# Memsets between indirect gathers: one of 512 elements behind every fourth gather instead of one of 128 behind each

## The chip, the core and the metric

The kernel runs on one core of a Trainium2 chip. The metric is the device time of one execution in microseconds (us). Lower is better. One execution was also recorded by the hardware profiler; the views below come from it. Engines are named as the profile names them: PE is TensorE, PEld its weight loads, DVE is VectorE, ACT is ScalarE, POOL is GpSimd, SP is SyncE, which here issues most of the plain transfers.

## The reference

A graph network of two attention layers with a layer norm ahead and a residual around it, on 6250 nodes of 256 features. There are 200000 edges, sorted by destination, with 32 features each. All data is float32. Cut to what matters:

```python
def _gat(x, src, dst, ea, Wg, a_s, a_d, Wge, a_e, b, n, h, f):
    hx = (x @ Wg).reshape(n, h, f)
    he = (ea @ Wge).reshape(-1, h, f)
    al = leaky_relu(einsum(hx, a_s)[src] + einsum(hx, a_d)[dst] + einsum(he, a_e), 0.2)
    m = segment_max(al, dst, num_segments=n)
    al = exp(al - m[dst])
    al = al / segment_sum(al, dst, num_segments=n)[dst]
    out = segment_sum(hx[src] * al[:, :, None], dst, num_segments=n)
    return out.reshape(n, h * f) + b

def _forward(x, edge_index, edge_attr, ...):
    src, dst = edge_index
    orig = x
    te = relu(edge_attr @ We0 + be0) * exp(x @ Wo0 + bo0)[src][:, None]
    s2, d2, ea2 = _add_self_loops(src, dst, te, n)
    x = relu(_gat(x, s2, d2, ea2, Wg0, ..., n, HEADS, PH) + x)      # 4 heads of 64
    te = relu(edge_attr @ We1 + be1) * exp(x @ Wo1 + bo1)[src][:, None]
    s2, d2, ea2 = _add_self_loops(src, dst, te, n)
    x = _gat(x, s2, d2, ea2, Wg1, ..., n, 1, D) + x                 # 1 head of 256
    return x + orig

h = maximum(_layernorm(x, axis=-1), 0.0)
x = x + _forward(h, edge_index, edge_attr_32, ...)
```

What the change touches is `hx[src]`: for each edge, the row of its source node is fetched from memory.

## The kernel before

The prologue normalises the nodes and writes a table `T` with one row per node: the node's 256 transformed features and a few numbers that the logits need (266 values in all in layer 0). While it does so, 24 gathers of the plain `x` rows (L243) fill the buffer `G0` for the first step; no memset follows these.

The 200000 edges are cut into 1563 chunks of 128, one edge per partition. A step has C = 24 chunks; a layer has 66 steps, of which the last two have 14 and 13 chunks. All edges of a step are sorted by destination, so its sums belong to at most 128 destination rows. The loop in `edges` goes over the steps of both layers. Its iteration k emits, in this order: the loads of the destination rows of step k+2 (`nodes`, L989), the load of the local row numbers `lb` of step k+2, now and then a load of further edge indices, the gathers of step k+1 (`gather`, L916), the logits and maxima of step k, the parts of step k+1 that depend on the edge features (`rphase1`, `rphase2`; L1014, L1019, L1028), the load of the edge features `ea` of step k+2, the scaling of the gathered rows by their weights (L1223), the sums (L1234), the one-hot matrices of the next step (L1058), the finish of step k-1 (`finish`, with the stores of rows to `T` or to the output in `rows3`), the eviction of the sums from PSUM (L1239), and the carry to the next step (L1245).

**The gathers.** `gather` issues one indirect transfer per chunk on Pool. Each fetches 128 rows of `T` into one slot of `G`, the last chunk's first, then chunks 0, 1, 2 and so on. `G` has three buffers that steps take in turn, so the first gather of a batch waits until the sums of an earlier step have read the buffer. Every gather also waits for the one that used its semaphore eight gathers before. Behind each gather, except in step 0, Pool writes zeros to a tile `gap` of 128 elements per partition (L932). Nothing reads `gap`.

**The sums.** For each chunk, a matmul of the one-hot matrix `S` (edges by destination rows) with the scaled rows `G` adds to one PSUM tile `u`: 24 in a step, 48 records in the profile. ScalarE then copies `u` to `U` (L1239). A step's end is told below by this copy.

**The destination rows.** `nodes` reads a row number into a register of SP and loads the 128 destination rows of a step from `T`, and in layer 0 those of `x` too, into the tile `tw` (522 elements per partition, five buffers). The row is loaded two steps ahead, and read last in the finish of its step, one iteration behind it. SP issues its transfers in the program's order. What stands behind `nodes` in SP's queue is `lb`, the index loads, the flags `fl`, the edge features `ea` and the row stores.

At the end of a layer, the last steps are emitted by `begin`, `tight` and `last` in an order of their own; in layer 1's first step, several batches of gathers follow each other without a pause.

Of the kernel before, what the change touches and what calls it, by code (L numbers as in the profile page):

```python
# [22 lines left out]
F32 = mybir.dt.float32  # L23
# [8 lines left out]
P = 128  # L32
# [3 lines left out]
D = 256  # L36
# [42 lines left out]
class Kernel:  # L79
# [317 lines left out]
    def fixed_rows(self):  # L397
        nc, cp = self.nc, self.cp
        self.crow = cp.tile([1, D + self.L[0].H], F32, name="crow")
        self.cl = [cp.tile([36, P + 1], F32, name=f"cl{i}") for i in range(2)]  # L400
        for t in self.cl:
            nc.gpsimd.memset(t, -BIG)

        self.cnt = cp.tile([P, self.NS, 2], F32, name="cnt")
        self.mt = cp.tile([P, 4 * C + 4], F32, name="mt")
        self.gap = cp.tile([P, 128], F32, name="gap")
        self.fb = [cp.tile([P, 37 * C], F32, name=f"fb{i}") for i in range(2)]
        for t in [self.mt] + self.fb:
            nc.gpsimd.memset(t, 0.0)


        self.aq = [cp.tile([P, 4, 32], BF, name=f"aq{i}") for i in range(2)]
        for t in self.aq:
            nc.gpsimd.memset(t, 0.0)
        self.trow1 = []
        L1 = self.L[1]
        for i in range(2):
            self.trow1.append(cp.tile([P, 2 * L1.TW], F32, name=f"t1row{i}"))
            nc.gpsimd.memset(self.trow1[i][:, L1.TW + D:], 0.0)
# [498 lines left out]
    def gather(self, st, c0=0, idx=None):  # L918
        nc, L = self.nc, st["L"]
        st["G"] = G = self.G0 if st["k"] == 0 else self.gp[st["k"] % 3].tile([P, C, 270], F32, name="G")  # L920
        n = self.N
        if idx is None:
            idx = self.src[:, st["o"]:st["o"] + st["C"]]
        else:
            n += P
        last = st["C"] - 1
        for c in (range(c0, last + 1) if c0 else (last, *range(last))):
            nc.gpsimd.indirect_dma_start(  # L928
                out=G[:, c, 0:L.TW], out_offset=None, in_=self.rows[L.l][0:n * (1 + L.l), :],
                in_offset=bass.IndirectOffsetOnAxis(ap=idx[:, c:c + 1], axis=0))  # L930
            if st["k"]:
                nc.gpsimd.memset(self.gap, 0.0)  # L932

    def pair(self, k):
# [54 lines left out]
    def nodes(self, st):  # L989
        nc, L, s = self.nc, st["L"], st["s"]  # L990
        r = self.row(0, s)
        tw = self.np_.tile([P, self.L[0].TW + D], F32, name="tw", bufs=5)
        st["tw"], st["xw"] = tw[:, :L.TW], tw[:, L.TW:L.TW + D]
        w = L.TW + L.l * D
        nc.sync.dma_start(tw[:, :w], self.T[L.l][ds(r, P), 0:w])
        if L.l == 0:
            nc.sync.dma_start(st["xw"], self.a["x"][ds(r, P), :])
# [402 lines left out]
    def general_layer(self, L, wp, pp):  # L1400
# [94 lines left out]
        with tc.For_i(0, full, P) as i:  # L1495
            nodes(i)
        if full < N:
            nodes(N - P)
# [98 lines left out]
```

## Time and profile before

| | |
|---|---|
| median of 3 runs | 4717.75 us (4715.25 to 4721.8) |
| the profiled execution | 4718.23 us |
| span of the recorded instructions in it | 4716.0 us |
| mean granted clock of TensorE | 0.732 |
| busy: POOL | 3701.8 us, 78% of the span |
| busy: PE / PEld | 3214.2 us, 68% / 1915.8 us, 41% |
| busy: DVE | 2878.5 us, 61% |
| busy: ACT | 574.2 us, 12% |
| gathers of L928 | 3102, 0.959 us each on Pool |
| memsets of L932 | 3102, 0.221 us each on Pool |
| one step, eviction to eviction | 34.6 us in layer 0, 34.4 us in layer 1 |

Some 2.2 us of the profiled execution lie outside its span. A row of the timeline is: start in us from the span's start, duration in us, engine, line, operation, the tile written and the tiles read, the shapes, the number of instructions in a row, and in brackets how long the engine had stood before it and what ended that. "issue" means that nothing in the profile was being waited for; "remote" means that the releaser was not among the recorded instructions. A row of the page's groups is: line, engine, operation, tiles, shapes, count, then total busy time in us and mean ns of one, then the engine's total idle time just before these and what ended most of it.

### The profile page before, as it was taken

What the parts mean: (1) busy time and instruction counts of PE and PEld (TensorE: products, weight loads), DVE (VectorE), ACT (ScalarE), POOL (GpSimd) and SP (SyncE); (2) the same over time, 40 slices, a digit from 0 to 9 for tenths busy, and PEclk for the clock granted to TensorE, in tenths of its full rate; (3) what the DMA queues carried; (4) which work ended last, traced back from release to release, by engine and by line L of the source; (5) the groups of instructions that cost most, each with busy time, mean ns of one, the idle gap of its engine ahead of it and who ended that gap; (6) DMA issues with size and microseconds to landing.
All of it is one profiled execution on the core that took longest, in us unless ns stands there. A gap on an engine that the chain in (4) does not pass through costs nothing.

```text
span 4716.0 us, 38255 instructions
## 1 busy us (share of the span) xinstructions
PE 3214.2 (68%) x10176; PEld 1915.8 (41%) x10176; DVE 2878.5 (61%) x6552; ACT 574.2 (12%) x1282; POOL 3701.8 (78%) x6350
## 2 busy tenths in 40 slices
PE   7777767777677776777655666666666666656666
PEld 6444444444444443444422333434333343433334
DVE  7566767667676676766743555546455555645555
ACT  5111111111111111111100001000000100000010
POOL 5688888888888888888648888888888888888884
PEclk9677777767777777777866677777767776777778
DMA  6344444444444444444323444444444444444442
GB/s 216 111 129 126 136 122 129 134 122 135 127 134 127 124 136 123 132 131 124 107 84 104 128 118 126 125 112 127 120 127 118 126 126 111 127 118 128 118 124 63
DMA packets 236364, 584.09 MB, mean 124 GB/s; under 512 B 63097, under 2 KB 91007, under 8 KB 236073
## 3 DMA queue, kind: packets, MB, share of 16 engines
q0 software_dynamic: 150144, 422.75, 33.8%
q1 hardware_dynamic: 85579, 158.16, 10.1%
q8 instruction: 82, 1.34, 0.1%
q14 instruction: 143, 1.17, 0.1%
q10 hardware_dynamic: 416, 0.67, 0.1%
HBM read 547.11 MB, written 34.33 MB: 123 GB/s over the span
## 4 chain that ended last, share of the span: by engine, by line
DVE 40%; another core or an unknown queue 33%; PE 16%; issue 6%; ACT 4%; POOL 0%; DMA 0%; SPq 0%; DVEq 0%; ACTq 0%; POOLq 0%
DVE G L1223 16%; DVE S L1058 8%; PE y L1014 8%; PE fin L1245 3%; DVE rt L1101 2%; ACT R L1019 1%; ACT U L1239 1%; DVE ade L1104 1%; PE fin L1329 1%; PE u L1234 1%; PE lf L1138 1%; PE zad L1028 1%; DVE mt L1172 1%; DVE m L1175 1%
## 5 line engine op out<-in xcount | busy, mean ns | idle before, releaser
L928 POOL DMA_INDIRECT G<-T,src x3102 | 2974.0, 959 | 938.3 <-issue 498.2
L1234 PE MATMUL u<-G,S 128*128 128x270 f32 (+1 forms) x6252 | 1469.7, 393 | 110.3 <-issue 58.0
L1234 PEld LDWEIGHTS u<-G,S 128*128 128x128 f32 x6252 | 1186.9, 192 | 394.5 <-issue 87.1
L1245 PE MATMUL fin<-U,lsel 128*1 128x270 f32 (+1 forms) x260 | 132.8, 613 | 1143.3 <-ACT U L1239 1136.6
L1223 DVE TENSOR_TENSOR G<-G,kps 128x6144 f32<-128x6144 f32 (+2 forms) x140 | 853.3, 6100 | 0.0
L1014 PE MATMUL y<-ea,webd 64*128 64x384 f32 (+1 forms) x1056 | 754.6, 866 | 89.2 <-issue 65.5
L932 POOL MEMSET gap<- 128x128 f32 x3102 | 684.6, 221 | 4.3 <-remote 1.3
L1148 DVE TENSOR_TENSOR_SCAN cl<-fl,cl,lf 4x129 f32<-4x129 f32 (+1 forms) x130 | 61.2, 471 | 1016.6 <-PE zad L1073 994.3
L1245 PEld LDWEIGHTS fin<-U,lsel 128*1 128x1 f32 x260 | 11.1, 81 | 1202.6 <-ACT U L1239 1201.5
L1028 PE MATMUL zad<-R,wea 128*64 128x384 f32 (+1 forms) x1056 | 474.0, 816 | 0.3 <-DVE aq L1080 0.3
L1014 PEld LDWEIGHTS y<-ea,webd 64*128 64x128 f32 x1056 | 303.3, 317 | 360.3 <-issue 330.0
L1058 DVE TENSOR_TENSOR S<-kps,loc 128x3072 f32<-128x3072 f32 x132 | 436.2, 3305 | 0.0
L1019 ACT ACTIVATE R<-y,webd 128x768 f32<-128x768 f32 x260 | 232.9, 896 | 794.6 <-PE y L1014 348.3
L1028 PEld LDWEIGHTS zad<-R,wea 128*64 128x64 f32 x1056 | 160.4, 207 | 314.9 <-issue 248.5
L1239 ACT ACTIVATE U<-u 128x270 f32<-128x270 f32 (+1 forms) x132 | 51.8, 393 | 1627.1 <-remote 1585.4
L1101 DVE STREAM_TRANSPOSE rt<-zad 128x768 f32<-128x768 f32 (+1 forms) x130 | 125.0, 961 | 27.8 <-remote 15.7
L424 PE MATMUL fin<-wg,h1T 128*128 128x260 f32 x264 | 135.7, 669 | 3.2 <-ACT h1T L1331 3.2
L1043 DVE TENSOR_TENSOR lb<-lb,kps 128x1536 bf16<-128x1536 bf16 (+1 forms) x68 | 113.0, 1662 | 0.0
L424 PE MATMUL ps<-wg,hT 128*128 128x266 f32 x292 | 89.8, 435 | 25.4 <-ACT hT L311 13.9
L424 PEld LDWEIGHTS fin<-wg,h1T 128*128 128x128 f32 x264 | 76.0, 317 | 53.7 <-issue 36.3
L1272 ACT ACTIVATE mw<-mw,mg 128x2 f32<-128x2 f32 x66 | 19.7, 298 | 557.3 <-DVE mw L1264 249.1
L1138 PE MATMUL lf<-ident,fb 128*36 128x128 f32 (+1 forms) x132 | 54.9, 416 | 42.8 <-DVE al L1119 28.2
(193 smaller groups left out, 2269.0 us busy)
## 6 DMA issues: line engine op xcount, KB each, us to landing
G<-T,src POOLq DMA_INDIRECT x3102
ea<-in_ea_dram SPq DMA_DIRECT2D x64, 768.0 KB
lb<-locrow SPq DMA_DIRECT2D x64, 384.0 KB
T<-t1row SPq DMA_DIRECT2D x66, 260.0 KB
tw<-T SPq DMA_DIRECT2D x66, 258.0 KB
tw<-T SPq DMA_DIRECT2D x66, 134.0 KB
tw<-in_x_dram SPq DMA_DIRECT2D x66, 128.0 KB
out_dram<-fb SPq DMA_DIRECT2D x64, 128.0 KB
```

Of the source, the lines that this page charges most:

```text
L424: self.nc.tensor.matmul(ps[:, :L.MW], hT[:, k, :], self.wg[L.l][:, k, :], start=(k == 0), stop=(k == 1))
L928: nc.gpsimd.indirect_dma_start(out=G[:, c, 0:L.TW], out_offset=None, in_=self.rows[L.l][0:n * (1 + L.l), :], in_offset=bass.IndirectOffset ...
L932: nc.gpsimd.memset(self.gap, 0.0)
L1014: nc.tensor.matmul(y[:, o], self.webd[l][r, :], ea[r, w], start=True, stop=True)
L1019: nc.scalar.activation(R[:, i, :32 * c].rearrange("p (b n) -> p b n", b=2), y.rearrange("p (b n) -> p b n", b=2)[:, :, :16 * c], AF.Relu, ...
L1028: nc.tensor.matmul(st["zad"][i * PH:(i + 1) * PH, o], self.wea[l][0], R[:, i, w], start=True, stop=False)
L1043: V.tensor_tensor(lb[:, :, :n], lb[:, :, :n], self.k_part.unsqueeze(2).to_broadcast([P, i, n]), op=OP.is_equal)
L1058: nc.vector.tensor_tensor(st["S"][:, c0:c1, :], self.k_iota.unsqueeze(1).to_broadcast(w), self.loc[:, o + c0:o + c1].unsqueeze(2).to_broad ...
L1101: V.transpose(rv[:, :32 * c].rearrange("p (b n) -> p b n", b=2), z.rearrange("p (b n) -> p b n", b=2)[:, :, :16 * c])
L1223: nc.vector.tensor_tensor(v, v, pw[:, c0:c1, :].unsqueeze(3) .to_broadcast([P, c1 - c0, H, L.F]), op=OP.mult)
L1234: nc.tensor.matmul(st["u"][:, :L.W], S[:, i, :], G[:, i, 0:L.W], start=(j == 0), stop=(j == c - 1))
L1245: nc.tensor.matmul(pr[0:1, :L.W], self.lsel[:, s:s + 1], U[:, :L.W], start=True, stop=True)
```

## The change

The memset behind a gather is emitted only where the chunk's number leaves 3 when divided by 4, and `gap` has 512 elements per partition instead of 128. In a full batch, whose gathers go in the order 23, 0, 1, ..., 22, the memsets stand behind the gathers of chunks 23, 3, 7, 11, 15 and 19. The tile `tw` has four buffers instead of five.

```diff
-        self.gap = cp.tile([P, 128], F32, name="gap")
+        self.gap = cp.tile([P, 512], F32, name="gap")
...
             nc.gpsimd.indirect_dma_start(
                 out=G[:, c, 0:L.TW], out_offset=None, in_=self.rows[L.l][0:n * (1 + L.l), :],
                 in_offset=bass.IndirectOffsetOnAxis(ap=idx[:, c:c + 1], axis=0))
-            if st["k"]:
+            if st["k"] and c % 4 == 3:
                 nc.gpsimd.memset(self.gap, 0.0)
...
-        tw = self.np_.tile([P, self.L[0].TW + D], F32, name="tw", bufs=5)
+        tw = self.np_.tile([P, self.L[0].TW + D], F32, name="tw", bufs=4)
```

## Prediction

> **What bounds the kernel now.** I read the page first: sections 1 and 5 for Pool.
>
> ```profile
> span 4716.0 us, 38255 instructions
> ...
> PE 3214.2 (68%) x10176; PEld 1915.8 (41%) x10176; DVE 2878.5 (61%) x6552; ACT 574.2 (12%) x1282; POOL 3701.8 (78%) x6350
> ...
> L928 POOL DMA_INDIRECT G<-T,src x3102 | 2974.0, 959 | 938.3 <-issue 498.2
> L932 POOL MEMSET gap<- 128x128 f32 x3102 | 684.6, 221 | 4.3 <-remote 1.3
> ...
> L1148 DVE TENSOR_TENSOR_SCAN cl<-fl,cl,lf 4x129 f32<-4x129 f32 (+1 forms) x130 | 61.2, 471 | 1016.6 <-PE zad L1073 994.3
> ```
>
> Pool has the largest share, and the memsets are 684.6 us of it. VectorE waits 994.3 us in front of L1148 for a matmul of TensorE, so VectorE has room. The question is whether Pool's own time sets the step. The timeline of one layer-0 step, and the start of a layer-1 step, answer it:
>
> ```profile
> 1015.11 0.40 ACT L1239 ACTIVATE U<-u 128x270 f32<-128x270 f32 x1 [9.56 <-remote]
> 1015.35 0.95 POOL L928 DMA_INDIRECT G<-T,src  x1 [2.36 <-remote]
> 1016.30 0.22 POOL L932 MEMSET gap<- 128x128 f32 x1
> 1016.69 0.95 POOL L928 DMA_INDIRECT G<-T,src  x1 [0.17 <-issue]
> ...
> 1046.22 0.95 POOL L928 DMA_INDIRECT G<-T,src  x1 [0.17 <-issue]
> 1047.17 0.22 POOL L932 MEMSET gap<- 128x128 f32 x1
> 1050.04 0.95 POOL L928 DMA_INDIRECT G<-T,src  x1 [2.65 <-remote]
> ...
> 2522.15 0.95 POOL L928 DMA_INDIRECT G<-T,src  x1 [3.04 <-remote]
> 2556.33 0.39 ACT L1239 ACTIVATE U<-u 128x261 f32<-128x261 f32 x1 [15.55 <-remote]
> ```
>
> A batch of 24 gathers starts at 1015.35, 0.24 us after ScalarE evicts the sums (U). It lasts 30.87 us to the start of its last gather, and then Pool stands for 2.65 us. The next batch starts at 1050.04, again just behind U. TensorE has issued its last sums at 1007.08, yet U comes at 1015.11. Its release seems to be held back until the gathers are cleared: U follows the start of the last gather by 3.3 us in 123 of the 132 steps, whether TensorE ended 7.7 us earlier (layer 0) or 10.3 us (layer 1).
>
> How long clearing takes is read from first gather to release. With 24 gathers it is 2556.33 - 2522.15 = 34.18 us. The batch of 13 at the end, and the 13 gathers of the prologue, which have no memset at all, give the rest:
>
> ```profile
> 4654.09 0.95 POOL L928 DMA_INDIRECT G<-T,src  x1 [8.63 <-PE u L1234]
> 4670.13 0.95 POOL L928 DMA_INDIRECT G<-T,src  x1 [0.17 <-issue]
> 4672.67 0.39 ACT L1239 ACTIVATE U<-u 128x261 f32<-128x261 f32 x1 [12.27 <-remote]
> ```
>
> ```profile
> 5.58 1.13 POOL L243 DMA_INDIRECT G<-in_x_dram,src  x1 [0.17 <-issue]
> 17.33 0.94 POOL L243 DMA_INDIRECT G<-in_x_dram,src  x1 [0.30 <-issue]
> 18.58 0.95 POOL L243 DMA_INDIRECT G<-in_x_dram,src  x1 [0.31 <-issue]
> 21.08 0.95 POOL L243 DMA_INDIRECT G<-in_x_dram,src  x1 [0.30 <-issue]
> 24.28 0.38 ACT L311 ACTIVATE hT<-pT 128x256 f32<-128x256 f32 x1 [2.07 <-PE ps L424]
> ```
>
> Thirteen with memsets take 4672.67 - 4654.09 = 18.58 us. So a gather costs (34.18 - 18.58) / 11 = 1.418 us, with 0.15 us left over. That is more than Pool's pitch of 0.95 + 0.22 + 0.165 = 1.335. Thirteen without a memset, at a pitch of 1.25, take 24.28 - 5.58 = 18.70: the same. Pool is done sooner there and the wait behind its last gather is longer (3.20 us against 2.54). Over the 117 steady steps the two also trade off: where a batch is 1 us longer, the wait behind it is 0.86 to 0.92 shorter, and the step grows by only 0.08 to 0.135. The step is set by something that serves gathers behind Pool at 1.418 us each, and the memset has no visible share in it.
>
> **The change part by part.** Of 24 gathers, 6 are followed by a memset (chunks 23, 3, 7, 11, 15, 19) instead of 24. It is of 512 elements.
>
> ```profile
> 2.95 1.62 POOL L409 MEMSET fb<- 128x888 f32 x2
> 4.86 0.55 POOL L233 MEMSET zero<- 128x536 f32 x1
> ```
>
> 888 elements take 0.81, 536 take 0.55, 128 take 0.22: I take 0.53 for 512. A gather without a memset behind it has the prologue's pitch of 1.25 (0.30 of it issue), so a small memset costs only 0.085 net. From first to last gather of a batch there are 23 intervals: 17 × 1.25 + 6 × (0.95 + 0.53 + 0.17) = 31.15 us, before 23 × 1.335 = 30.71. Pool's batch gets 0.44 us longer, although its memset time falls to about 6 × 0.53 = 3.2 us a step from 5.3. The last gather then starts 34.18 - 31.15 = 3.0 us ahead of the expected release. Its packets end 2.45 us behind its start, so about half a microsecond of cover stays. If it is gone, the step grows by what is missing.
>
> What the step pays has two bounds. By the trade-off above, 0.44 × 0.08 to 0.135 = 0.035 to 0.06 us, times 129 (3102 gathers / 24): +5 to +8 us. Below, 18 instructions fewer: layer 0's step has 36 instructions more than layer 1's and is 0.2 us longer, so an instruction is worth at most 0.0056 us; 18 × 0.0056 × 129 = -13 us. The prologue, where a memset less saved nothing, is the nearest row, and lies between. I take 0.
>
> The gathers land some 20 to 30 us before their logits; only layer 1's first batch is waited for. There the batch's 0.44 us is exposed: +0.4 us.
>
> A rule of the Trainium skill speaks against the longer memset: "SBUF — State Buffer", section "Who interferes with whom", has VectorE in its two-port modes and GpSimd exclude each other for a whole instruction. By it a VectorE operation meets a memset less often (6 × 0.53 against 24 × 0.22 of 34.6 us) but waits longer, half its length: as an estimate 0.024 against 0.017 us, for some 8 such operations +0.06 us a step, or +7 us. In this trace VectorE's scale (6.54 us) and one-hots (3.35 us) last the same at each of their occurrences beside gathers and memsets, so I add nothing for it.
>
> Four row buffers instead of five: the loads of step k+2 now wait until VectorE has last read step k-2's rows, in the step shown at 1005.4 instead of the 997.7 at which the load is issued now. Behind the waiting load on SP's queue stand lb, the index loads, fl, ea and the stores of T or of the output. tw and lb are read an iteration later, the others at least 10 us later: cost 0. Were that cover gone, each microsecond of lateness would cost 132 us over the steps. Pool's queue is not moved.
>
> Sum: 4718.23 (the profiled run: span 4716.0 and 2.2 around it) + 0 + 0.4. The median 4717.75 is 0.5 under that run, so I forecast 4718.
>
> **The rivals.**
> - Instruction count counts: Pool, or whatever serves semaphores behind it, is freed by 18 instructions a step. For it: layer 1's shorter step. Against it: the prologue. -13 us, 4705; if a memset holds as much as 0.01 us of the 1.418, 24 × 0.01 × 129 = -31, some 4687.
> - Pool paces the step after all: U follows the last gather by a fixed 3.3 us. For it: 123 steps of 132. Against it: the trade-off, and 3.20 against 2.54 us above. 0.44 × 129 = +57, 4774. It decides if the cover of half a microsecond is used up.
> - Bunching chokes the others. From the moment the sums end, layer 0's VectorE is held up in quanta of 0.70 us until the batch is cleared. Four gathers at 1.25, well under 1.418, pile up more at once than an even 1.335. One quantum more in each of the last three bunches is 2.1 us; the wait before L1148 that must absorb it was 1.12 us in the step above and 3.76 in the one before. Half the steps of layer 0 lose 1 us: 64 × 0.5 = +32, 4750. It decides where that wait falls to zero. Against it: after four gathers the pause of 0.53 brings the mean pitch back to 1.354.
> - U is released in the longer pauses, and Pool no longer waits: a step of 32.4 + 0.2, or 4460. The prologue speaks against it: held results came there at 15.69 and 21.34 in the middle of the batch, but the batch was cleared no sooner.
> - The change does nothing but move Pool's memsets: that is the forecast itself.
>
> **How the numbers follow.** A measurement of this kernel can tell about 0.2%, 9.4 us, from no change. Forecast (nothing, up to +8): 0.36. Instruction count or a small share of the memset (4687 to 4705): 0.25. Pauses that release U: 0.05. Pool paces: 0.12. Bunching: 0.18, and 0.04 for a heavier choke above 4775. So faster 0.30, same 0.36, slower 0.34. Leaving out the 4460 case and the heavy choke, the range is 4690 to 4775. The likeliest case's own range is 4710 to 4728.
>
> **What would show it.** Right: 774 memsets (6 for each full batch, 3 for each of the four short ones) near 0.53 us; a pitch of 1.25 within a bunch; last gather some 31.2 us behind the first; the wait from it to U down to about 2.9; steps still 34.6 and 34.4 us. Wrong: first gather to U away from 34.2 while the wait stays 3.3 (Pool paces), stalls of 0.70 us on VectorE ahead of the sums' end, a wait before L1148 near zero, U ahead of the last gather, or SP's tw load as a releaser of VectorE.

## The result and the profile after

The changed kernel takes 4787.59 us (median of 4 runs, 4784.57 to 4792.31), the kernel before 4717.47 us in the same comparison: a ratio of 1.015, 95% interval 1.0135 to 1.0165. That is 70 us slower, and outside the range forecast. The profiled execution has a span of 4787.6 us, against 4716.0.

The page's rows of the changed kernel, beside those shown of the kernel before:

```profile
span 4787.6 us, 36019 instructions
...
PE 3254.5 (68%) x10176; PEld 1929.2 (40%) x10176; DVE 2866.8 (60%) x6552; ACT 573.8 (12%) x1282; POOL 3427.5 (72%) x4022
...
L928 POOL DMA_INDIRECT G<-T,src x3102 | 2960.2, 954 | 1285.9 <-issue 792.7
L932 POOL MEMSET gap<- 128x512 f32 x774 | 420.7, 544 | 0.2
```

Pool's busy time fell by 274 us, and the kernel became slower. There are 774 memsets, as worked out, at 544 ns (530 were forecast). The same step of layer 0 as before, from the timeline:

```profile
1019.71 0.40 ACT L1239 ACTIVATE U<-u 128x270 f32<-128x270 f32 x1 [9.79 <-remote]
1019.94 0.94 POOL L928 DMA_INDIRECT G<-T,src  x1 [2.48 <-remote]
1020.25 0.63 DVE L1070 CAST a<-a3r 128x4 bf16<-128x4 f32 x1
1020.87 0.55 POOL L932 MEMSET gap<- 128x512 f32 x1
1021.59 0.95 POOL L928 DMA_INDIRECT G<-T,src  x1 [0.17 <-issue]
1022.84 0.95 POOL L928 DMA_INDIRECT G<-T,src  x1 [0.30 <-issue]
```

The second gather starts 1.65 us after the first; it was 1.34 before. From there on the pitch is 1.25 within a bunch. The step's shape is as before, but each step of layer 0 is 0.19 us longer (34.79 against 34.60 on average).

Layer 1 has something new. Two steps in a row:

```profile
2998.05 0.94 POOL L928 DMA_INDIRECT G<-T,src  x1 [2.65 <-remote]
...
3026.49 0.54 POOL L932 MEMSET gap<- 128x512 f32 x1
...
3028.45 0.95 POOL L928 DMA_INDIRECT G<-T,src  x1 [0.30 <-issue]
3029.53 0.39 ACT L1239 ACTIVATE U<-u 128x261 f32<-128x261 f32 x1 [13.01 <-remote]
3029.70 0.95 POOL L928 DMA_INDIRECT G<-T,src  x1 [0.30 <-issue]
3030.95 0.95 POOL L928 DMA_INDIRECT G<-T,src  x1 [0.30 <-issue]
...
3051.43 0.98 DVE L1101 STREAM_TRANSPOSE rt<-zad 128x768 f32<-128x768 f32 x1 [6.42 <-remote]
3062.30 0.95 POOL L928 DMA_INDIRECT G<-T,src  x1 [0.30 <-issue]
3062.92 0.59 PE L1234 MATMUL u<-G,S 128*128 128x261 f32 x1 [2.45 <-issue]
3065.72 5.42 PE L1234 MATMUL u<-G,S 128*128 128x261 f32 x11 [2.20 <-issue]
3071.17 0.39 ACT L1239 ACTIVATE U<-u 128x261 f32<-128x261 f32 x1 [14.14 <-PE u L1234]
```

U is evicted at 3029.53, ahead of the batch's last gather (3029.70) and 3.04 us behind the start of the memset that follows the 21st gather. Pool then has no rest: the next batch starts at 3030.95, one pitch behind. The step was only 31.72 us long. But the next one waits for results all along (6.42 us before L1101, where steps outside such pairs wait for nothing) and takes 41.64 us. In it TensorE's sums are held up too: TensorE stands 1 to 2.5 us before single matmuls, with nothing in the profile that they wait for, as in the two PE rows above. Waits of more than 0.5 us add up to 8.8 us on average within the sums of such a long step, and to 0.4 in the other steps of layer 1. Together the two steps are 73.36 us, 4.6 more than two of 34.40. There are 13 such pairs in layer 1, worth 52 us in all.

So, from eviction to eviction: +11.3 us over the 60 full steps of layer 0, +57.3 in layer 1, of which 52 in the pairs, and +2.9 in the start, the change of layers and the tail. That is 71.5 us.

### The profile page after: what moved, and what is told of

It is laid out like the page before. It is cut to its first block, busy times and chain, and to the rows that moved or that the text cites. A ratio compares the mean times of both kernels' runs of the same rounds, so it can differ in the third digit from the quotient of the medians.

```text
span 4787.6 us, 36019 instructions
## 1 busy us (share of the span) xinstructions
PE 3254.5 (68%) x10176; PEld 1929.2 (40%) x10176; DVE 2866.8 (60%) x6552; ACT 573.8 (12%) x1282; POOL 3427.5 (72%) x4022
## 3 DMA queue, kind: packets, MB, share of 16 engines
q0 software_dynamic: 150144, 422.75, 34.1%
q8 instruction: 82, 1.34, 0.1%
## 4 chain that ended last, share of the span: by engine, by line
DVE 30%; another core or an unknown queue 21%; PE 19%; POOL 16%; issue 11%; ACT 3%; DMA 1%; DVEq 0%; POOLq 0%; ACTq 0%; SPq 0%
POOL G L928 13%; DVE G L1223 12%; PE y L1014 6%; PE u L1234 6%; DVE S L1058 6%; PE fin L1245 2%; POOL gap L932 2%; DVE rt L1101 2%; PE zad L1028 1%; PE fin L1329 1%; PE ps L424 1%; ACT U L1239 1%; DVE mt L1172 1%; DVE ade L1104 1%
## 5 line engine op out<-in xcount | busy, mean ns | idle before, releaser
L1234 PE MATMUL u<-G,S 128*128 128x270 f32 (+1 forms) x6252 | 1530.3, 401 | 235.9 <-issue 180.3
L1234 PEld LDWEIGHTS u<-G,S 128*128 128x128 f32 x6252 | 1212.6, 196 | 554.3 <-issue 213.4
L1223 DVE TENSOR_TENSOR G<-G,kps 128x6144 f32<-128x6144 f32 (+2 forms) x140 | 853.1, 6099 | 0.0
L1014 PE MATMUL y<-ea,webd 64*128 64x384 f32 (+1 forms) x1056 | 731.7, 843 | 112.3 <-ACT R L1019 62.8
L1028 PE MATMUL zad<-R,wea 128*64 128x384 f32 (+1 forms) x1056 | 484.4, 820 | 20.6 <-issue 13.0
L932 POOL MEMSET gap<- 128x512 f32 x774 | 420.7, 544 | 0.2
L1101 DVE STREAM_TRANSPOSE rt<-zad 128x768 f32<-128x768 f32 (+1 forms) x130 | 125.0, 961 | 131.4 <-remote 120.3
L1169 DVE SCALAR_TENSOR_TENSOR m<-fpen,lf,m 128x24 f32<-128x24 bf16 (+1 forms) x66 | 16.3, 247 | 115.8 <-PE lf L1155 56.9
```

The source lines that it names most:

```text
L1014: nc.tensor.matmul(y[:, o], self.webd[l][r, :], ea[r, w], start=True, stop=True)
L1028: nc.tensor.matmul(st["zad"][i * PH:(i + 1) * PH, o], self.wea[l][0], R[:, i, w], start=True, stop=False)
L1101: V.transpose(rv[:, :32 * c].rearrange("p (b n) -> p b n", b=2), z.rearrange("p (b n) -> p b n", b=2)[:, :, :16 * c])
L1223: nc.vector.tensor_tensor(v, v, pw[:, c0:c1, :].unsqueeze(3) .to_broadcast([P, c1 - c0, H, L.F]), op=OP.mult)
L1234: nc.tensor.matmul(st["u"][:, :L.W], S[:, i, :], G[:, i, 0:L.W], start=(j == 0), stop=(j == c - 1))
```

## Experiments

Two theories stood against each other at first: the grouped pauses themselves, or the fourth row buffer. `gap` is read by nothing, so a changed memset changes no result. The kernel before was run on each chip beside the others. It took 4713 us on one chip, 4766 and, some 19 minutes later, 4717 us on a second, and 4380 to 4385 us on three others. On the latter, U starts 0.4 us behind the start of TensorE's last matmul instead of 8 to 11 us, and Pool never rests. Each ratio below is against runs on the same chip at the same time; "late" and "at once" name the two kinds of chip.

**Four row buffers alone.**

```diff
-name="tw", bufs=5
+name="tw", bufs=4
```

> Only the row buffers go from five to four; a memset of 128 stays behind every gather. Pause theory (the grouped, longer memset lets the sums' release through ahead of the batch's end in layer 1, Pool then runs on without its rest of 3.2 us, and the next step is choked): 4717 to 4722, every step as before. Buffer theory (the row load that now waits for the finish delays lb, fl and the stores on SP's queue into a worse place): 4770 to 4790, with the same pairs of a 31.7 us and a 41.6 us step in layer 1.

> Four row buffers alone, once more, because the first chip of the experiments ran the kernel before in 4380 us with the sums released at once. On a chip where the sums are released late (kernel before at 4700 to 4770): no change within 5 us by the pause and the pitch theory; 20 us or more slower by the buffer theory. On a chip that releases at once: about 10 us faster, as measured there.

At once: 4369.22 against 4379.73 us (0.9977, 0.9968 to 0.9987). Late: 4717.40 against 4713.25 (1.001, 1.000 to 1.002). The row buffers cost at most some 9 us, and layer 1 shows no pair. The buffer theory falls.

**Grouped pauses alone**, five row buffers, `gap` of 144 elements.

```diff
-            if st["k"]:
+            if st["k"] and c % 4 == 3:
+                nc.gpsimd.memset(self.gap, 0.0)
                 nc.gpsimd.memset(self.gap, 0.0)
```

> Five row buffers as before; two memsets of 144 elements, together as long as one of 512 (0.55 us), behind every fourth gather. Pause theory: 4775 to 4800, with the pairs of short and long steps in layer 1. Buffer theory: 4717 to 4735, no pairs.

> Grouped memsets (two of 144 behind every fourth gather), five row buffers. On a chip with late release: +20 us or more (0.2 us for each of 128 steps, as in the pair of traces 4763.0 and 4786.8), and +60 to +75 if steps with an early release appear in layer 1. By the buffer theory: no change. On a chip that releases at once: +4 us, as measured.

At once: 4383.57 against 4379.73 (1.001, 1.0001 to 1.002). Late: 4747.61 against 4713.25 (1.0073, 1.0056 to 1.009). The loss on the late chip follows the pauses. Its layer 1 had no pairs; its layer 0 had four short steps followed by a long one (26.99 and 42.29 us, for instance).

**Grouped in layer 0 only**, an edit of the changed kernel.

```diff
-            if st["k"] and c % 4 == 3:
+            if st["k"] and L.l:
+                nc.gpsimd.memset(self.gap[:, :128], 0.0)
+            elif st["k"] and c % 4 == 3:
```

> The changed kernel with its grouped memset of 512 in layer 0 alone; in layer 1 one of 128 behind each gather again; four row buffers. If the loss splits as the steps of the two traces say, 0.19 us a step stay in layer 0 (+12 us) and nothing in layer 1: 4727 to 4733. If layer 1's loss comes from the four row buffers: 4775 to 4790.

4387.85 against 4379.73 us (1.0018, 1.0009 to 1.0028), but at once, where the changed kernel's pairs cannot be told apart. Inconclusive for the split.

**No memset at all.**

> No memset at all, five row buffers. Pause theory: no pause, so no early release; 24 gathers are cleared 34.2 us behind the first one as in the prologue, layer 1 stays at 34.4 us a step, and the time is 4710 to 4740. Bunching theory (gathers at a pitch of 1.25 us choke VectorE and TensorE by themselves, and the spacing by memsets is what prevents it): layer 0 and layer 1 both lose more than in the changed kernel, over 4800.

> No memset. On a chip with late release, if gathers are cleared at their own 1.42 to 1.43 us each whatever Pool does: 34.2 us from first gather to release as before, within 15 us of the kernel before. If Pool's pitch sets it after all: 24 x 1.25 = 30 us a step, over 250 us faster, as on the chip that releases at once. If bunching chokes: slower, above 4800.

At once: 4090.86 against 4379.73 us (0.9342, 0.9326 to 0.9357). Steps average 29.7 and 30.0 us, which is 24 gathers at 1.25: there Pool's pitch is the bound, and 3102 memsets cost 289 us, 0.093 us each. Late: 4858.47 against 4713.25 (1.0316, 1.0298 to 1.0333), the opposite sign. Clearing still takes 34 us or more although Pool is done in 29, and the timeline of the late chip shows TensorE's sums held up in the middle (first view; the second is a step of the kernel before):

```profile
1007.67 3.12 PE L1232 MATMUL u<-G,S 128*128 128x270 f32 x13
1012.81 0.39 PE L1232 MATMUL u<-G,S 128*128 128x270 f32 x1 [2.01 <-issue]
1015.62 0.61 PE L1232 MATMUL u<-G,S 128*128 128x270 f32 x1 [2.42 <-issue]
1023.85 0.40 ACT L1237 ACTIVATE U<-u 128x270 f32<-128x270 f32 x1 [8.52 <-PE u L1232]
```

```profile
996.14 11.33 PE L1234 MATMUL u<-G,S 128*128 128x270 f32 x48 [0.33 <-issue]
```

Single matmuls come 2.8 us apart, with nothing in the profile that they wait for; the kernel before issues all 48 in 11.3 us. Such waits of more than 0.5 us come to 8.4 us in a step without memsets and 0.5 in a step of the kernel before. Spacing the gathers is what keeps TensorE running there.

**The kernel before and the changed one once more**, on a late chip.

> The kernel before once more, for its trace on the chip of this call. If the chip sets the mode (sums released late and Pool resting 3.2 us behind each batch, or sums released at once and Pool running without a rest), its steps are all of one kind: 34.4 to 34.6 us and some 4717 us, or 24 x 1.335 = 32.0 us on average and some 4380 us. If the mode is struck anew in each execution, both kinds appear among the executions of one kernel.

> The changed kernel against the one before on the chip of this call. Where the sums are released late: 1.015 as in the first result. Where they are released at once, Pool paces the step: 24 gathers take 18 x 1.25 + 6 x 1.65 = 32.4 us against 32.05, so +0.35 us a step, 132 steps, +46 us at most (1.010), and about +4 us (1.001) if it goes as with the two memsets of 144 behind every fourth.

The kernel before took 4765.1 us, the changed one 4789.24 against 4766.21 (1.0048, 1.0031 to 1.0065). Layer 0's step grew from 34.93 to 35.15, layer 1's from 34.74 to 34.93, and there is no pair. So the loss has two parts: about 0.2 us in each step, in both comparisons, and the pairs, which come or stay away. The chip alone does not decide on them: later, on this same chip, the changed kernel had 13 again (below).

**The pauses moved by two gathers**: behind the 3rd, 7th, ..., 23rd gather, an edit of the changed kernel.

```diff
-            if st["k"] and c % 4 == 3:
+            if st["k"] and c % 4 == 1:
```

> The changed kernel with the memset behind chunks 1, 5, ..., 21 instead of 3, 7, ..., 19 and 23. The last pause then lies behind the 23rd gather, not the 21st. Pause theory, on a chip with late release: an early release comes 3.0 us behind that memset, when all 24 gathers are out, so Pool cannot run on without a rest: no pairs of a 31.7 and a 41.6 us step, and only the +0.2 us a step (about +23 us). If the loss hangs on four gathers in a row, and not on where the pause is: the same as the changed kernel on the same chip.

Late: 4712.77 against 4713.25 us (0.9997, 0.9988 to 1.0007). Two pairs are left (32.8 and 39.3 us, 32.9 and 40.2). The whole loss is gone, the 0.2 us a step too, which the pause theory had let stay. What this kernel no longer has is a pause behind the first gather. That gave the queue theory: as in the prediction, something serves gathers one by one behind Pool at 1.418 us; as long as Pool's pitch is shorter, work is always waiting; but with the second gather 1.65 us behind the first, nothing else is queued, and 0.23 us of service are lost.

**The changed kernel, the same without its first memset, and the kernel before with a long first one**, all on the chip that gave 4766 us before. The second edit is shown against the kernel before; it also has four row buffers and a `gap` of 512.

```diff
-            if st["k"] and c % 4 == 3:
+            if st["k"] and c % 4 == 3 and c < last:
```

```diff
             if st["k"]:
-                nc.gpsimd.memset(self.gap, 0.0)
+                nc.gpsimd.memset(self.gap if c == last else self.gap[:, :128], 0.0)
```

> The changed kernel once more, as the measure for the other kernels of this call on the same chip. On a chip with late release: +0.2 us in every step (+23 us), and some +45 us more if layer 1 shows the pairs of an early release and a long step behind it.

> The changed kernel without the memset behind each batch's first gather; the five behind chunks 3 to 19 stay. Queue theory (gathers are served one after another at 1.418 us each; a pause of 0.70 us behind the first gather makes the second come at 1.65 us, when nothing else is queued, and 1.65 - 1.418 = 0.23 us of service are lost in each step): layer 0's step returns from 34.79 to 34.6 us, the +23 us are gone; pairs in layer 1 stay if the pause behind the 21st gather makes them. Theory that four gathers in a row make the step longer: no gain against the changed kernel, or a loss, since five now go in a row.

> A memset of 128 behind each gather as before, but of 512 behind each batch's first one; four row buffers. Queue theory: 1.65 - 1.418 = 0.23 us more a step, +28 us (1.006) on a chip with late release, no pairs. Bunching theory: nothing is bunched, so no change (within 5 us).

All late, against 4716.80 us: the changed kernel 4796.75 (1.0171, 1.0153 to 1.0189) with 13 pairs again; without the first memset 4701.59 (0.997, 0.9958 to 0.9983), no pair; the long first memset alone 4753.21 (1.008, 1.0063 to 1.0096), one pair. One memset in six makes the difference of 95 us, pairs included. The starts of two batches, first without and then with it:

```profile
1009.46 0.95 POOL L928 DMA_INDIRECT G<-T,src  x1 [2.41 <-remote]
1010.71 0.95 POOL L928 DMA_INDIRECT G<-T,src  x1 [0.31 <-issue]
...
1043.63 0.40 ACT L1239 ACTIVATE U<-u 128x270 f32<-128x270 f32 x1 [9.49 <-remote]
```

```profile
1019.71 0.95 POOL L928 DMA_INDIRECT G<-T,src  x1 [2.04 <-remote]
1020.66 0.54 POOL L932 MEMSET gap<- 128x512 f32 x1
1021.37 0.95 POOL L928 DMA_INDIRECT G<-T,src  x1 [0.17 <-issue]
```

Medians over the full batches, in us, of the time between the first two gathers and from the first gather to U, in traces of several late chips. In the comparison at 4766 us, which is not in the table, the first gather to U took 34.61 before and 34.79 changed.

| kernel | first two gathers | first gather to U |
|---|---|---|
| before | 1.335 | 34.23 |
| moved by two gathers | 1.249 | 34.21 |
| changed, without first memset | 1.252 | 34.13 |
| grouped, two of 144 | 1.607 | 34.43 |
| changed | 1.648 | 34.50 |
| long first memset alone | 1.655 | 34.53 |

Where the second gather comes before 1.418, clearing takes 34.1 to 34.2; where it comes later, by 0.19 to 0.24, it takes 0.2 to 0.3 us more.

**A memset of 256 behind each gather**, five row buffers.

> A memset of 256 (about 0.33 us) behind each gather, five row buffers: Pool's pitch rises from 1.335 to about 1.445 us, above the 1.418 of the service. Queue theory: nothing piles up any more, the sums' release follows TensorE's last matmul within 0.5 us instead of 8 to 11 us, Pool has no rest behind a batch, and a step is 24 x 1.445 = 34.7 us: 4715 to 4760. If the late release has nothing to do with Pool's pitch: the release stays 3 us behind the last gather, and a step is 23 x 1.445 + 3.3 + 0.24 = 36.8 us, some 4990.

On a late chip, as the kernel before beside it shows: 4711.10 against 4716.80 us (0.9988, 0.9978 to 0.9998), 4 us under the range expected. The timeline:

```profile
964.80 5.18 PE L1234 MATMUL u<-G,S 128*128 128x270 f32 x22
...
969.92 0.33 POOL L932 MEMSET gap<- 128x256 f32 x1
970.02 0.40 ACT L1239 ACTIVATE U<-u 128x270 f32<-128x270 f32 x1 [1.93 <-PE u L1234]
970.41 0.95 POOL L928 DMA_INDIRECT G<-T,src  x1 [0.17 <-issue]
```

With the pitch at 1.45 us, above the service, U starts 0.42 us behind the start of the last matmul, Pool has no rest, and the steps average 34.5 and 34.9 us: 24 pitches. So the late release behaves as a queue that is fed faster than it is served. This kernel is not faster in earnest, since 24 services or 24 pitches are nearly the same.

What is queued is not the rows themselves. At each of the 24 places of a batch, 95 in 100 of a gather's transfer packets have ended 2.4 to 2.6 us behind its start (medians), in the kernel before, in the one without memsets on the late chip, and on a chip that releases at once: nothing piles up there. Something else goes with the late release, which the experiments did not look at: records are missing from the trace. Each landing of a gather is recorded 16 times in the trace of the four row buffers on a chip that releases at once; in that of the kernel before it is 12.7 times on average for a batch's first gather and 2 to 4 from the eighth on. With the memset of 256 it is 6 to 16 times. So the recording itself is crowded just when results are late, and may be what holds them up. Each execution of the experiments has a span of recorded instructions on record, so no run here tells the two apart, and what is served at 1.418 us stays open.

**The last three** meant to settle the pairs and the 15 us gain of the kernel without the first memset:

```diff
+if st["k"] and c % 4 == 3 and c != last - 4:    # changed kernel, no memset behind the 21st gather
+if st["k"] and c < last:                        # kernel before, no memset behind the first gather
+if st["k"] and c % 2 and c < last:              # 256 behind every second, none behind the first
```

> The changed kernel without the memset behind the 21st gather (chunk 19); the pause behind the first gather stays. Queue theory: the first pause still loses 0.23 us a step, +25 to +30 us. If the pairs in layer 1 come from a release in the pause behind the 21st gather, 3.0 us ahead of it, they are gone, and +25 to +30 is all; if they come from the lost 0.23 us alone, wherever the pauses are, they stay, and the time is +60 to +85.

> The kernel before without the memset of 128 behind each batch's first gather, all others kept. Queue theory: the second gather comes at 1.25 instead of 1.335 us, both ahead of 1.418, so nothing is lost or won: within 5 us of the kernel before. If a first gather without any memset behind it is a gain by itself: -15 us, as in the changed kernel without its first memset.

> A memset of 256 behind chunks 1, 3, ..., 21: 11 for 24 gathers, none behind the first gather, five row buffers; mean pitch 1.34 us. Queue theory with a small price for each memset (19 fewer gave about 0.1 to 0.15 us a step): no loss from a pause, 13 fewer memsets, -8 to -12 us. Without such a price: within 5 us.

> The changed kernel without the memset behind the 21st gather once more, since the call before fell on the chip that releases the sums at once. On a chip with late release (kernel before at 4700 to 4770): +25 to +30 us and no pairs in layer 1 if the pairs come from a release in that last pause; +60 to +85 us with pairs if the 0.23 us lost behind the first gather bring them wherever the pauses are.

All fell on chips that release at once, where no queue builds: 4355.98 (0.9946, 0.9929 to 0.9962), 4364.70 (0.9966, 0.9952 to 0.998) and 4377.77 (0.9993, 0.9984 to 1.0003) against 4381.56 us; the first again 4361.00 against 4384.55 (0.9939, 0.9922 to 0.9956). The first has four row buffers, which alone gave 10.5 us on such a chip; the second leaves out one memset of 24 and gains 17 us; the third, with 11 longer memsets, gains nothing clear. They say nothing on the late kind, so whether a first gather without a memset is a gain there stays untested by itself. What makes a release come early in layer 1 stays open: the kernels with four or more pairs all have a second gather later than 1.6 us (though the changed kernel had none in the comparison at 4766 us), and the one kernel that differs from the changed kernel only there has none, but how the lost 0.23 us lead to them was not shown.

## Why the prediction was wrong

- **Its mechanism was right, and carried further than the forecast used it.** "Something that serves gathers behind Pool at 1.418 us each" fits the runs: the pitch of 1.45 releases at once, and leaving all memsets out does not shorten the clearing. What that something is was not shown; the rows' transfers it is not.
- **The step that failed is "What the step pays ... I take 0".** It compared the mean pitch of a batch, 1.354, with the service, and bounded the price by the trade-off between a batch's length and the wait behind it: +5 to +8 us. It did not run the batch through its own queue gather by gather. The pause behind chunk 23 stands behind the *first* gather, where nothing is queued: 1.65 - 1.418 = 0.23 us lost, times 129 is +30 us. The long first memset alone measured +36 us, with one pair in it. In the changed kernel the term measured 0.19 us a step in layer 0. Pool's batch grew by 0.43 us, as forecast (0.44), but the wait behind it fell only from 3.30 to 3.19 us, not to 2.9. The trade-off had been read from batches in which a delay fell where a queue stood: of 150 delays of over 0.03 us between gathers in the kernel before, 101 lie behind the 16th and the 19th gather, and one behind the first.
- **The rival "U is released in the longer pauses" happened, with the other sign.** The prediction priced it as a gain of 2 us in every step. The release came early in 13 steps, which gained 2.4 us on average, and the steps behind them lost 6.4 (2.7 and 7.2 in the pair shown). That is +52 of the +70 us, and nothing in the forecast held it. That the loss comes from Pool skipping its rest of 3 us is argued from the order of events, not shown; a plain queue does not give it, since 48 gathers at 1.418 would be cleared in 68.1 us, and the pair took 73.1 from its first gather to the second U.
- **"Pool paces the step after all"** (+57, 4774) came close in size and is not what happened: the kernel with moved pauses has as long a batch as the changed one (31.4 us to its last gather against 31.3) and loses nothing.
- **"Bunching chokes the others"** is real without any pause (TensorE held up on the late chip). Five gathers in a row alone do not do it: the changed kernel without its first memset has them and is the fastest of the kernels run on the late chips. But the long steps of the pairs show the same sign, 8.8 us of waits within TensorE's sums. The rival had put its loss on VectorE, in half of layer 0's steps, and had not tied it to an early release.
- **Held:** the memset's 0.53 us (0.544), the pitch of 1.25, the longer batch, and the row buffers at nothing (+4 us, 0 to +9).
- **The exclusion of VectorE and GpSimd is there, but small.** The prediction looked for it in the scale and the one-hots, and the scale's mean is unchanged (6099 ns against 6100). These are TENSOR_TENSOR operations, for which the section it names of the Trainium skill ("SBUF — State Buffer", section "Who interferes with whom") gives no two-port mode. Casts show it: in the step above the CAST of L1070 starts inside a gather and lasts 0.63 us, until that gather ends, where its median is 0.18 (at most 0.72). By these times it is the gather that blocks there, not the memset. On average this cast became 31 ns longer in layer 0, and that of L1068 36 ns shorter, so nothing of the estimated +7 us is seen.
- **The 13 us for fewer instructions** stay unsettled: the kernel without the first memset has 19 fewer in a step and is 15 us faster, the one with moved pauses has 18 fewer and is not, of which its two pairs explain 7.8 us.

## What to carry to other kernels

Where a producer runs ahead of something that serves its requests, the mean pitch decides little: a pause costs its excess over the service time where the queue is empty, at the start of a batch, and little where work is waiting. So keep the first pause away from the first request; here leaving out that one, so that the first pause stood behind the fifth gather, turned +80 us into -15, and pauses from the third gather on cost nothing. And a result that comes early and lets the producer run on without a rest can make the next step longer than it made this one shorter. All of this was seen with the profiler recording; whether it holds without it was not tried.

## What was not expected of the hardware

The same kernel takes 4713 to 4766 us on some chips and 4380 to 4385 on others. By the queue theory the service of a gather is some 1.42 us on the first and at most 1.25 on the second. A change of the gathers' spacing can therefore have either sign: without memsets, -6.6% on one chip and +3.2% on another. While gathers are queued on a late chip, ScalarE and Pool see the end of TensorE's sums up to 11 us late, although these sums read rows that were gathered a batch earlier. The trace does not tell whether the sums end late there or only their report comes late, and its missing records leave open that the recording has a part in it.
